# Attention over 16 graphs: ScalarE in written order, and the weights' passes spread over the bursts

## The chip, the core and the metric

The kernel runs on one core of a Trainium2 chip. A core has TensorE (matmul, PE in the profile, with its weight loads as PEld), VectorE (DVE), ScalarE (ACT), GpSimd (POOL), and queues that issue DMA transfers (SP for most of them here). Each engine has its own list of instructions, and semaphores tie the lists together. The metric is the device time of one execution in microseconds (us), from the first to the last instruction, as a median of several executions.

## What is computed

Sixteen graphs of 1024 nodes with 256 features pass through two layers. Only the first layer is touched by the change. For each graph it builds an attention whose queries come from a product with an adjacency matrix weighted by the graph itself:

```python
fea = jnp.transpose(x, (0, 2, 1))
c_adj = jnp.mean(fea, axis=1)                          # mean of a node's features
diff = c_adj[:, None, :] - c_adj[:, :, None]
A = jnp.abs(jnp.abs(jax.nn.sigmoid(diff) - 0.5) - 0.5) * 2.0
A_s = (A + jnp.transpose(A, (0, 2, 1))) * 0.5
Wg = adj[None, :, :] * A_s                             # the graph's weights, 1024 x 1024
g = jax.nn.relu(jnp.einsum('bcn,bnm->bcm', fea, Wg) * para.reshape(1, C, N))
q = jnp.transpose(g, (0, 2, 1)).reshape(B, N, h, hd).transpose(0, 2, 1, 3)
kv = (x @ kv_w).reshape(B, N, 2, h, hd).transpose(2, 0, 3, 1, 4)
attn = jax.nn.softmax(jnp.einsum('bhnd,bhmd->bhnm', q, kv[0]) * scale, axis=-1)
out = jnp.einsum('bhnm,bhmd->bhnd', attn, kv[1])       # 4 heads of 64
# then: x = layernorm(x + out), and a second layer (graph product, two linear
# layers with batch norm, layernorm)
```

All data is float32. With t = tanh(|difference of means| / 2) the weights are (up to the sign, which the kernel puts into the scale of q) `(t - 1) * adj`.

## The kernel before

The first layer is written as a software pipeline. While TensorE works on the attention of graph b, the queries, keys and values of graph b+1 are made between its bursts, and the transposes and first weights of graph b+2. A unit is 128 keys by 512 queries for two heads; a graph has 32 units, and a burst is two of them, so a graph has 16 bursts, numbered u = 0 to 15 below.

```python
with (
    ...
    tc.tile_pool(name="xp", bufs=3) as xp,        # x of three graphs
    tc.tile_pool(name="crp", bufs=1) as crp,
    tc.tile_pool(name="wgp", bufs=NCH) as wgp,    # the 8 weights tiles of one graph
    tc.tile_pool(name="pp", bufs=4) as pp,        # exponentials of four units
    ...
):
# PSUM pools, two tiles each: ps_s (scores), ps_t (everything of the block
# steps, transposes and denominators), ps_o (attention output)
```

The work for a graph's queries, keys and values comes in three lists: `first` (transposes of x), `steps` (block steps: values, keys, graph product) and `side` (the weights' passes).

```python
def prologue(b):
    ...
    def begin():
        ...
        nc.vector.tensor_reduce(csum, xt, AX.X, ALU.add)          # needs x loaded
        ...                                                        # ccol, ncol
        nc.sync.dma_start(c_d[b].rearrange("o (n p) -> p (o n)", p=P), ncol)
        s["crow"] = crp.tile([P, N], F32, tag="crow", name=f"crow_{b}")
        nc.sync.dma_start(s["crow"], c_d[b][0].partition_broadcast(P))

    def transpose_x(c, half):
        if c == 0 and half == 0:
            begin()
        pt = tile_t(f"pxT_{b}_{c}_{half}")
        ...                                                        # 4 transposes
        nc.vector.tensor_copy(s["xT"][:, c, half * HALF : (half + 1) * HALF], pt)

    def weights_abs(n):
        w = wgp.tile([P, N], F32, tag="wg", name=f"wg_{b}_{n}")
        nc.scalar.activation(w, s["crow"], AF.Abs, bias=s["ccol"][:, n : n + 1])
        s["wg", n] = w

    def weights_tanh(n):
        w = s["wg", n]
        nc.scalar.activation(w, w, AF.Tanh, scale=0.5)
        nc.vector.scalar_tensor_tensor(
            w, w, 1.0, adj_s[:, n, :], op0=ALU.subtract, op1=ALU.mult
        )

    def graph_mm(c, half, part):                                   # 2 of 8 matmuls
        ...
        if part == 3:
            q = s["qT"][:, c, hs]
            nc.vector.scalar_tensor_tensor(
                q, ps, -scale, para_s[:, c, hs], op0=ALU.mult, op1=ALU.mult
            )
            nc.scalar.activation(q, q, AF.Relu)

    def keys(kc, half):
        ...
        nc.scalar.copy(s["kT"][:, kc, hs], ps)

    def values(pair):
        ...
        nc.vector.tensor_copy(
            s["v"][:, 2 * pair : 2 * pair + 2, :].rearrange("p n c -> p (n c)"), pt
        )
    ...
    for n in range(NCH):
        side.append((weights_abs, (n,)))
        side.append((weights_tanh, (n,)))
    return first, steps, side
```

A unit's attention is a score product, an exponential on ScalarE, an output product, and a running sum of the exponentials on VectorE:

```python
def scores(i):
    ps = tile_s(f"ps_{i}")
    ...                                                            # 4 matmuls into ps
    p = pp.tile([P, N], F32, tag="p", name=f"p_{i}")
    nc.scalar.activation(p, ps, AF.Exp)

def outputs(i):
    ...                                                            # 4 matmuls with p
    nc.vector.tensor_add(g["acc"], g["acc"], p)                    # first: p0 + p
    if m == NCH - 1:                                               # every 8th unit
        nc.scalar.copy(g["oT"], g["po"][0])
        nc.vector.tensor_add(g["oT"], g["po"][1], g["oT"])

def residual(b, pr, qh):
    ...                                                            # transposes of oT
    nc.vector.tensor_mul(o, ...)                                   # by 1 / denominator
    nc.gpsimd.tensor_tensor(xs, xs, o.rearrange("p n h d -> p n (h d)"), ALU.add)
    if pr == PAIRS - 1 and qh == 1:                                # last of the graph
        layernorm(s["x"], f"l0_{b}")
        nc.gpsimd.dma_start(x1_d[b], s["x"])
        del st[b]
```

The main loop. Inside `manual_schedule` the engines that are named issue in the order of writing; a scheduler orders the others, ScalarE among them.

```python
FULL = {0: 4, 4: 4, 6: 4, 8: 4, 10: 4, 12: 4}
with tc.manual_schedule(engines={mybir.EngineType.PE}):
    ...
    for j in range(len(bursts)):
        b, u = j // PERB, j % PERB
        for i in bursts[j]:
            scores(i)
        run(quarter.get(j, []), 9)                 # denominators
        if u == 0:
            steps, side = next_steps, next_side
            next_first, next_steps, next_side = [], [], []
        if u == 5 and b + 2 < B:
            load_x(b + 2)
            next_first, next_steps, next_side = prologue(b + 2)
        if j:
            back(j - 1)                            # outputs of the burst before
        if u in FULL:
            run(full.get(j, []), 9)                # residuals
            run(steps, FULL[u])
            if u >= 10:
                run(next_first, 2)
        if u > 12:
            run(next_side, 2)
        else:
            run(side, 1 if u in FULL else 2)
```

Of the kernel before, what the change touches and what calls it, by code (L numbers as in the profile page):

```python
# [515 lines left out]
def fast_path(  # L516
# [19 lines left out]
    nc = tc.nc  # L536
# [3 lines left out]
    NCH = N // P  # L540
# [15 lines left out]
    def tile_t(name):  # L556
        return ps_t.tile([P, HALF], F32, tag="t", name=name)
# [4 lines left out]
    x1_d = [dram.tile([P, NCH, C], F32, tag=f"x1_{b}", name=f"x1_{b}") for b in range(B)]  # L562
# [11 lines left out]
    def rsqrt(dst, src, eps):  # L574
        n = dst.shape[1]
        if eps:
            nc.gpsimd.tensor_scalar(dst, src, eps, None, ALU.add)  # L577
            src = dst
        nc.gpsimd.tensor_tensor(dst, src, mhalf[:, :n], ALU.pow)  # L579

    def layernorm(t, name):
        st = small.tile([P, NCH, 6], F32, tag="ln_st", name=f"st_{name}")
        mv = small.tile([P, NCH, 2], F32, tag="ln_mv", name=f"mv_{name}")
        rstd = small.tile([P, NCH], F32, tag="ln_rs", name=f"rs_{name}")
        for n in range(NCH):
            nc.vector.bn_stats(st[:, n, :], t[:, n, :])
            nc.vector.bn_aggr(mv[:, n, :], st[:, n, :])
        rsqrt(rstd, mv[:, :, 1], EPS)
        for n in range(NCH):
            nc.vector.tensor_scalar(  # L590
                t[:, n, :], t[:, n, :], mv[:, n, 0:1], rstd[:, n : n + 1], ALU.subtract, ALU.mult
            )
# [20 lines left out]
    with (  # L613
# [15 lines left out]
        st = {}  # L629

        def load_x(b):
            t = xp.tile([P, NCH, C], F32, tag="x", name=f"x_{b}")
            nc.sync.dma_start(t, x[b].rearrange("(n p) c -> p n c", p=P))
            st[b] = {"x": t}
# [7 lines left out]
        def prologue(b):  # L642


            s = st[b]
            xt = s["x"]
            first, steps, side = [], [], []
# [34 lines left out]
            def weights_tanh(n):  # L682
                w = s["wg", n]
                nc.scalar.activation(w, w, AF.Tanh, scale=0.5)  # L684
                nc.vector.scalar_tensor_tensor(  # L685
                    w, w, 1.0, adj_s[:, n, :], op0=ALU.subtract, op1=ALU.mult
                )
# [57 lines left out]
            for n in range(NCH):  # L745
                side.append((weights_abs, (n,)))
                side.append((weights_tanh, (n,)))
            return first, steps, side


        PAIRS = H // 2
# [8 lines left out]
        def scores(i):  # L760
            b, pr, qh, m = units[i]
            qT, kT = st[b]["qT"], st[b]["kT"]
            ps = tile_s(f"ps_{i}")
            for kh in range(2):
                for hd in range(2):
                    r = slice(hd * D, (hd + 1) * D)
                    ks = slice(m * P + kh * D, m * P + (kh + 1) * D)
                    nc.tensor.matmul(  # L768
                        ps[kh * D : (kh + 1) * D, hd * HALF : (hd + 1) * HALF], kT[r, pr, ks],
                        qT[r, pr, qh * HALF : (qh + 1) * HALF], start=True, stop=True,  # L770
                    )
            p = pp.tile([P, N], F32, tag="p", name=f"p_{i}")
            nc.scalar.activation(p, ps, AF.Exp)  # L773
            A[i] = p

        def outputs(i):
            b, pr, qh, m = units[i]
            s, p = st[b], A.pop(i)
            if m == 0:
                G[b, pr, qh] = {  # L780
                    "po": [tile_o(f"po_{i}_{kh}") for kh in range(2)],
                    "acc": accp.tile([P, N], F32, tag="acc", name=f"acc_{i}"),
                }
            g = G[b, pr, qh]
            for hd in range(2):
                h = 2 * pr + hd
                for kh in range(2):
                    r = slice(kh * D, (kh + 1) * D)
                    nc.tensor.matmul(  # L789
                        g["po"][kh][hd * D : (hd + 1) * D, :], s["v"][r, m, h * D : (h + 1) * D],  # L790
                        p[r, hd * HALF : (hd + 1) * HALF], start=(m == 0), stop=(m == NCH - 1),
                    )
            if m == 0:
                g["p0"] = p
            elif m == 1:
                nc.vector.tensor_add(g["acc"], g.pop("p0"), p)
            else:
                nc.vector.tensor_add(g["acc"], g["acc"], p)  # L798
            if m == NCH - 1:
                k = (b * PAIRS + pr) * 2 + qh  # L800
                g["oT"] = op.tile([P, HALF], F32, tag="oT", name=f"oT_{k}")
                nc.scalar.copy(g["oT"], g["po"][0])
                nc.vector.tensor_add(g["oT"], g["po"][1], g["oT"])
# [25 lines left out]
        def residual(b, pr, qh):  # L829
            g, s = G.pop((b, pr, qh)), st[b]  # L830
            k = (b * PAIRS + pr) * 2 + qh
            nc.vector.reciprocal(r_all[:, k], g["col"])
            pt = tile_t(f"poT_{k}")
            for j in range(4):
                nc.tensor.transpose(
                    pt[:, j * P : (j + 1) * P], g["oT"][:, j * P : (j + 1) * P], ident
                )
            o = rdp.tile([P, 4, 2, D], F32, tag="o", name=f"o_{k}")
            nc.vector.tensor_mul(  # L839
                o, pt.rearrange("p (n h d) -> p n h d", h=2, d=D),  # L840
                r_all[:, k].unsqueeze(3).to_broadcast([P, 4, 2, D]),
            )
            xs = s["x"][:, 4 * qh : 4 * qh + 4, pr * P : (pr + 1) * P]
            nc.gpsimd.tensor_tensor(xs, xs, o.rearrange("p n h d -> p n (h d)"), ALU.add)  # L844
            if pr == PAIRS - 1 and qh == 1:
                layernorm(s["x"], f"l0_{b}")
                nc.gpsimd.dma_start(x1_d[b], s["x"])
                del st[b]

        def run(fs, k):  # L850
            for f, a in fs[:k]:
                f(*a)
            del fs[:k]
# [1 line left out]

        FULL = {0: 4, 4: 4, 6: 4, 8: 4, 10: 4, 12: 4}
        BURST = 2
        bursts = [range(i, i + BURST) for i in range(0, len(units), BURST)]  # L860
        PERB = PER // BURST
        with tc.manual_schedule(engines={mybir.EngineType.PE}):
            load_x(1)
            first, steps, side = prologue(0)
            run(first, 4)
            while steps:
                run(side, 4)
                run(steps, 2)
            next_first, next_steps, next_side = prologue(1)
            run(next_first, 4)  # L870
            run(next_side, 6)
            full, quarter = {}, {}

            def back(j):

                for i in bursts[j]:
                    outputs(i)
                b, pr, qh, m = units[bursts[j][-1]]
                if m == NCH - 1:
                    quarter.setdefault(j + 2, []).append((normalise, (b, pr, qh)))  # L880
                    k = j + 5
                    while k % PERB not in FULL:
                        k += 1
                    full.setdefault(k, []).append((residual, (b, pr, qh)))

            for j in range(len(bursts)):
                b, u = j // PERB, j % PERB
                for i in bursts[j]:
                    scores(i)
                run(quarter.get(j, []), 9)  # L890
                if u == 0:
                    steps, side = next_steps, next_side
                    next_first, next_steps, next_side = [], [], []
                if u == 5 and b + 2 < B:
                    load_x(b + 2)
                    next_first, next_steps, next_side = prologue(b + 2)
                if j:
                    back(j - 1)
                if u in FULL:
                    run(full.get(j, []), 9)  # L900
                    run(steps, FULL[u])
                    if u >= 10:
                        run(next_first, 2)
                if u > 12:
                    run(next_side, 2)
                else:
                    run(side, 1 if u in FULL else 2)
            j = len(bursts)
            back(j - 1)
            for k in range(j, j + 8):  # L910
                run(quarter.get(k, []), 9)
                run(full.get(k, []), 9)

        top = l0c.tile([P, 2], F32, name="top")
        nc.vector.tensor_reduce(top[:, 0:1], r_all, AX.XYZ, ALU.max)
# [275 lines left out]
```

## Time and profile before

| | |
|---|---|
| time, median of 3 | 2997.59 us (2993.03 to 2997.8) |
| span of the profiled execution | 2990.3 us |
| PE busy | 2736.4 us (92%) |
| DVE busy | 1418.0 us (47%) |
| ACT busy | 1138.6 us (38%) |
| POOL busy | 185.7 us (6%) |
| first score matmul of graph 0, last of graph 15 | 81.2 us, 1862.2 us |
| one exponential (L773) x512 | 1018 ns |
| one weights pass on ScalarE: Abs (L679) x128, Tanh (L684) | 1137 ns, 1045 ns |
| one weights product on VectorE (L685) x128 | 1220 ns |
| one running sum (L798) x384 | 1226 ns |

A busy time is the union of an engine's instructions. A row of the profile's slices gives the busy share in tenths for each fortieth of the span. An entry of the timeline gives the start, the length, the engine, the line of the kernel, the operation, and what it writes and reads; in brackets stands how long the engine was idle before it and who released it. Tiles are named as in the kernel: `ps` scores, `p` exponentials, `wg` weights, `pg` the graph product, `pv` and `pk` values and keys, `pxT` the transposes of x.

### The profile page before, as it was taken

The page shows a single profiled execution, that of the slowest core. Times are in us where ns is not written, and L with a number is a line of the kernel's source. Part 1 is how long each engine was busy: PE and PEld are TensorE (multiplying, and loading weights), DVE is VectorE, ACT ScalarE, POOL GpSimd, SP SyncE. Part 2 cuts the span into 40 slices and gives each one's busy share as a digit, 9 for nine tenths or more (in the row PEclk, how much of TensorE's full clock was granted, in tenths as well). Part 3 has the DMA queues.
Part 4 walks back from the last instruction along what each step waited for, and adds up shares of the span by engine and source line. Part 5 has one row for each costly group of instructions (what it writes and reads, how often), then busy time and mean ns, then how long its engine had stood idle before and what let it go on. Part 6 is the DMA issues. An engine that isn't in the chain of part 4 may idle for free. (4 is left out here: it accounts for less than half of the span.)

```text
span 2990.3 us, 32734 instructions
## 1 busy us (share of the span) xinstructions
PE 2736.4 (92%) x13522; PEld 1202.2 (40%) x13522; DVE 1418.0 (47%) x2130; ACT 1138.6 (38%) x1313; POOL 185.7 (6%) x196
## 2 busy tenths in 40 slices
PE   6999999999999999999999999799999999999842
PEld 3433334333333333334333333544444444344432
DVE  3565555655655665655655647511111212233464
ACT  3555354553553553553544535001101111233383
POOL 0000000000000000000000001000000000000032
PEclk9999999999999999999999999699999999999955
DMA  4001101101101001011011010022121220244265
GB/s 134 8 1 36 36 1 36 30 8 36 29 8 37 29 8 37 10 28 36 1 36 36 1 49 24 29 84 112 57 84 71 84 84 32 123 159 150 84 211 198
DMA packets 122062, 169.00 MB, mean 57 GB/s; under 512 B 86704, under 2 KB 103600, under 8 KB 111664
## 3 DMA queue, kind: packets, MB, share of 16 engines
q1 hardware_dynamic: 112720, 99.70, 10.9%
q0 software_dynamic: 9184, 67.12, 5.7%
q8 instruction: 108, 1.77, 0.3%
q14 instruction: 50, 0.41, 0.0%
HBM read 99.36 MB, written 67.44 MB: 56 GB/s over the span
## 5 line engine op out<-in xcount | busy, mean ns | idle before, releaser
L773 ACT ACTIVATE p<-ps 128x1024 f32<-128x1024 f32 x512 | 498.7, 1018 | 275.5 <-PE ps L768 263.6
L768 PE MATMUL ps<-qT,kT 64*64 64x512 f32 x4096 | 519.1, 619 | 69.6 <-ACT p L773 69.6
L798 DVE TENSOR_TENSOR acc<-acc,p 128x1024 f32<-128x1024 f32 x384 | 470.7, 1226 | 187.9 <-ACT p L773 174.8
L789 PE MATMUL po<-p,v 64*64 64x512 f32 x4096 | 500.4, 599 | 0.0
L697 PE MATMUL pg<-wg,x 128*128 128x512 f32 x1024 | 454.4, 597 | 4.3 <-ACT kT L718 4.3
L1003 PE MATMUL pagg<-ahT,x1l 128*128 128x512 f32 x1024 | 444.0, 593 | 0.0
L1022 ACT ACTIVATE hw<-ph,col_b 128x1024 f32<-128x1024 f32 x64 | 71.2, 1113 | 652.7 <-PE ph L1018 652.7
L768 PEld LDWEIGHTS ps<-qT,kT 64*64 64x64 f32 x4096 | 150.9, 137 | 368.1 <-issue 234.2
L1003 PEld LDWEIGHTS pagg<-ahT,x1l 128*128 128x128 f32 x1024 | 194.3, 190 | 241.1 <-issue 241.1
L697 PEld LDWEIGHTS pg<-wg,x 128*128 128x128 f32 x1024 | 190.2, 190 | 246.3 <-issue 216.6
L789 PEld LDWEIGHTS po<-p,v 64*64 64x64 f32 x4096 | 166.3, 137 | 292.8 <-issue 289.6
L1082 PE MATMUL po<-hl,w2T 128*128 128x512 f32 x512 | 222.8, 598 | 6.9 <-ACT hl L1073 6.9
L1018 PE MATMUL ph<-agg,w1T 128*128 128x512 f32 x512 | 222.2, 592 | 0.0
L1007 DVE COPY agg<-pagg 128x1024 f32<-128x1024 f32 x32 | 39.1, 1223 | 377.9 <-PE pagg L1003 377.9
L706 ACT ACTIVATE qT<-qT 128x512 f32<-128x512 f32 x64 | 40.1, 626 | 407.3 <-DVE qT L703 407.3
L685 DVE SCALAR_TENSOR_TENSOR wg<-wg,adj_s 128x1024 f32<-128x1024 f32 x128 | 153.3, 1220 | 77.0 <-ACT wg L684 77.0
L844 POOL TENSOR_TENSOR x<-x,o 128x512 f32<-128x512 f32 x64 | 81.1, 1267 | 1670.3 <-DVE o L839 1670.3
L1024 DVE BATCH_NORM_STATS2 bn_st<-hw 128x6 f32<-128x512 f32 x128 | 82.3, 685 | 152.4 <-ACT hw L1022 152.4
L727 PE MATMUL pv<-kvw_s,xT 128*128 128x256 f32 x512 | 128.0, 394 | 26.8 <-DVE v L731 16.1
L1082 PEld LDWEIGHTS po<-hl,w2T 128*128 128x128 f32 x512 | 98.3, 192 | 131.4 <-issue 121.9
L679 ACT ACTIVATE wg<-crow,ccol 128x1024 f32<-128x1024 f32 x128 | 140.8, 1137 | 17.2 <-PE pg L697 11.9
L1018 PEld LDWEIGHTS ph<-agg,w1T 128*128 128x128 f32 x512 | 97.3, 190 | 122.5 <-issue 122.5
(87 smaller groups left out, 1962.8 us busy)
## 6 DMA issues: line engine op xcount, KB each, us to landing
h<-hw POOLq DMA_DIRECT2D x16, 2048.0 KB, 6.6
hl<-h SPq DMA_DIRECT2D x16, 2048.0 KB
x<-in_x_dram SPq DMA_DIRECT2D x16, 1024.0 KB
x<-x POOLq DMA_DIRECT2D x16, 1024.0 KB, 4.3
x1l<-x SPq DMA_DIRECT2D x16, 1024.0 KB
xf<-x SPq DMA_DIRECT2D x16, 1024.0 KB
out_dram<-xf POOLq DMA_DIRECT2D x16, 1024.0 KB, 5.4
crow<-c SPq DMA_DIRECT2D x16, 512.0 KB
```

The lines of the kernel that those rows point to most:

```text
L679: nc.scalar.activation(w, s["crow"], AF.Abs, bias=s["ccol"][:, n : n + 1])
L685: nc.vector.scalar_tensor_tensor(w, w, 1.0, adj_s[:, n, :], op0=ALU.subtract, op1=ALU.mult)
L697: nc.tensor.matmul(ps, xt[:, n, c * P : (c + 1) * P], s["wg", n][:, hs], start=(n == 0), stop=(n == NCH - 1),)
L727: nc.tensor.matmul(pt[:, j * C : (j + 1) * C], s["xT"][:, c, n * P : (n + 1) * P], kvw_s[:, c, C : 2 * C], start=(c == 0), stop=(c == CC - 1),
L768: nc.tensor.matmul(ps[kh * D : (kh + 1) * D, hd * HALF : (hd + 1) * HALF], kT[r, pr, ks], qT[r, pr, qh * HALF : (qh + 1) * HALF], start=Tr ...
L773: nc.scalar.activation(p, ps, AF.Exp)
L789: nc.tensor.matmul(g["po"][kh][hd * D : (hd + 1) * D, :], s["v"][r, m, h * D : (h + 1) * D], p[r, hd * HALF : (hd + 1) * HALF], start=(m = ...
L798: nc.vector.tensor_add(g["acc"], g["acc"], p)
L1003: nc.tensor.matmul(ps[:, hs], xt[:, m, c * P : (c + 1) * P], ahT[:, m, hs], start=(m == 0), stop=(m == NCH - 1),)
L1018: nc.tensor.matmul(ps[:, hs], w1T[:, c, k * P : (k + 1) * P], t[:, c, hs], start=(c == 0), stop=(c == CC - 1),)
L1024: nc.vector.bn_stats(bn1_st[:, k, 2 * b + half, :], ht[:, k, half * HALF : (half + 1) * HALF])
L1082: nc.tensor.matmul(ps[:, hs], w2T[:, k, c * P : (c + 1) * P], ht[:, k, hs], start=(k == 0), stop=(k == HC - 1),)
```

## The change

ScalarE is added to the engines that issue in the order of writing. So the places at which the weights' passes are written now count, and they are chosen anew: one pass between plain bursts (`SIDE`), and pairs of them between the single block steps of bursts 0 and 4. The product with the adjacency matrix (VectorE) becomes an entry of its own in the list `side`, one weights tile behind the passes. The layer normalisation of a finished graph moves from its last residual to the burst after, ahead of the load of the next x. In bursts 10 and 12 one of the two transposes of x goes ahead of the four graph matmul steps. At the start six entries of `side` are written for each two steps, in place of four. The purpose is to keep passes from standing ahead of exponentials that TensorE waits for.

```diff
@@ weights_tanh
                 nc.scalar.activation(w, w, AF.Tanh, scale=0.5)
+
+            def weights_adj(n):
+                w = s["wg", n]
                 nc.vector.scalar_tensor_tensor(
                     w, w, 1.0, adj_s[:, n, :], op0=ALU.subtract, op1=ALU.mult
                 )
@@ the list side
                 side.append((weights_abs, (n,)))
                 side.append((weights_tanh, (n,)))
+                if n:
+                    side.append((weights_adj, (n - 1,)))
+            side.append((weights_adj, (NCH - 1,)))
@@ residual
-            if pr == PAIRS - 1 and qh == 1:
-                layernorm(s["x"], f"l0_{b}")
-                nc.gpsimd.dma_start(x1_d[b], s["x"])
-                del st[b]
+
+        def finish_x1(b):
+            xt = st.pop(b)["x"]
+            layernorm(xt, f"l0_{b}")
+            nc.gpsimd.dma_start(x1_d[b], xt)
@@ main
-        FULL = {0: 4, 4: 4, 6: 4, 8: 4, 10: 4, 12: 4}
+        FULL = (0, 4, 6, 8, 10, 12)
+        SIDE = {13: 1, 14: 1, 15: 1, 1: 1, 2: 1, 3: 1, 5: 4}
-        with tc.manual_schedule(engines={mybir.EngineType.PE}):
+        with tc.manual_schedule(engines={mybir.EngineType.PE, mybir.EngineType.Activation}):
             ...
             while steps:
-                run(side, 4)
+                run(side, 6)
                 run(steps, 2)
             next_first, next_steps, next_side = prologue(1)
             run(next_first, 4)
-            run(next_side, 6)
-            full, quarter = {}, {}
+            run(next_side, 4)
+            full, quarter, late = {}, {}, {}
@@ back, where the residual is placed in burst k
                     full.setdefault(k, []).append((residual, (b, pr, qh)))
+                    if pr == PAIRS - 1 and qh == 1:
+                        late.setdefault(k + 1, []).append((finish_x1, (b,)))
@@ loop over the bursts
+                if j:
+                    back(j - 1)
+                run(late.get(j, []), 9)
                 if u == 5 and b + 2 < B:
                     load_x(b + 2)
                     next_first, next_steps, next_side = prologue(b + 2)
-                if j:
-                    back(j - 1)
                 if u in FULL:
                     run(full.get(j, []), 9)
-                    run(steps, FULL[u])
                     if u >= 10:
-                        run(next_first, 2)
-                if u > 12:
-                    run(next_side, 2)
+                        run(next_first, 1)
+                    for _ in range(4):
+                        run(steps, 1)
+                        if u <= 4:
+                            run(side, 2)
+                    if u >= 10:
+                        run(next_first, 1)
+                elif u > 12:
+                    run(next_side, SIDE[u])
                 else:
-                    run(side, 1 if u in FULL else 2)
+                    run(side, SIDE.get(u, 0))
             ...
                 run(full.get(k, []), 9)
+                run(late.get(k, []), 9)
```

## The prediction

> **What bounds the kernel now.** I read the engines' busy shares and the clock row first, then the table of stretches, the waits of TensorE, and last the timeline of one graph. The page says where to look:
>
> ```profile
> PE 2736.4 (92%) x13522; PEld 1202.2 (40%) x13522; DVE 1418.0 (47%) x2130; ACT 1138.6 (38%) x1313; POOL 185.7 (6%) x196
> ...
> PE   6999999999999999999999999799999999999842
> ```
>
> TensorE is the bound, but 92% busy hides time: a stretch at half clock counts as busy. So I cut the attention stage into its 16 graphs at the first score matmul of each. Graphs 1 to 13 take 113.9 to 119.3 us, mean 115.4, graph 0 takes 110.6. Graph 14 prepares no successor's weights and takes 105.0. The stretches of graph 8, of graph 14, and of two pieces inside graph 8 (columns: length, busy time of PE, PEld, DVE, ACT, POOL, then clock, DMA share, GB/s):
>
> ```profile
> 1000.83:1115.83 115.00, 108.81 (x692) 44.71 (x688) 68.04 (x92) 55.66 (x64) 7.62 (x7) 0.97 0.09 24
> 1692.62:1797.63 105.01, 103.97 (x676) 42.24 (x672) 50.94 (x74) 39.68 (x48) 7.61 (x7) 1.00 0.12 41
> 1103.57:1109.94 6.37, 1.92 (x21) 0.52 (x13) 4.35 (x5) 6.37 (x9) 0.00 (x0) 0.85 0.08 1
> 1109.94:1114.82 4.88, 4.88 (x24) 1.54 (x28) 4.24 (x6) 2.90 (x3) 0.00 (x0) 0.50 0.00 0
> ```
>
> In the third row TensorE stands while ScalarE is full; in the fourth it works at clock 0.50. ScalarE's timeline tells why:
>
> ```profile
> 1103.95 1.06 ACT L684 ACTIVATE wg<-wg 128x1024 f32<-128x1024 f32 x1
> 1104.91 2.18 ACT L679 ACTIVATE wg<-crow,ccol 128x1024 f32<-128x1024 f32 x2
> 1106.99 1.99 ACT L684 ACTIVATE wg<-wg 128x1024 f32<-128x1024 f32 x2
> 1108.88 1.91 ACT L773 ACTIVATE p<-ps 128x1024 f32<-128x1024 f32 x2
> ...
> 1109.94 3.69 PE L768 MATMUL ps<-qT,kT 64*64 64x512 f32 x16 [4.45 <-ACT p L773]
> ```
>
> Five weights passes stand ahead of the exponentials, so the next scores find no free PSUM tile for 4.45 us. A stall of 4.45 or 4.46 us stands at burst 15 of each of graphs 0 to 13, 14 times.
>
> **What the Trainium skill says.** "TensorE: Matmul & The Clock Gate", section "What's actually happening": the array falls to half clock after an idle window of about 3.4 us and comes back after a busy one; the windows run free. The trace agrees: half-clock pieces are 3.41 or 6.83 us long in this stage. They also follow shorter stalls: one of 2.07 us (graph 2) brought 3.41 us of half clock, one of 1.42 us (graph 5) none. "ScalarE: Activation LUTs", section "Table sets: the hidden batching unit": exp, tanh, abs and relu lie in one set, so interleaving them loads no table. The trace agrees: one table load, 1.28 us, in the whole run. "Perfetto Trace Analysis", section "Sequencer Loop": an engine's instruction waits for its semaphores in the queue, behind it the rest. That makes the order on an engine the thing to read, and I read it in the compiled order of both programs.
>
> **Part 1: weights passes spread out.** A plain burst repeats every 3.43 us (score starts 1020.01, 1023.44). ScalarE spends 1.94 on two exponentials, so 1.5 are free: one pass of 1.05 to 1.14 fits, two don't. The change puts one pass in each of bursts 13, 14, 15, 1 and 2 and the other eleven in the block steps of bursts 0 and 4. In burst 0 TensorE has 7.4 us of block work; ScalarE then has oT copy 0.58, four passes 4.2, two kT copies 1.16, but waits for the first keys. Followed through, the exponentials of burst 1 start 0.5 to 1.0 us late; in burst 4 five passes fit after the keys and those of burst 5 start at about 1037.5 instead of 1035.9. The scores of burst 6 need the first at 1039.2 and it ends at 1038.5: it holds with 0.7 us. So the 14 stalls go: 14 x 4.45 = 62. The half clock after them goes too. In graph 8 it is 4.88 x 0.5 = 2.4; from the spacing of matmul starts in all 14 it is 2.3 in the mean: 14 x 2.3 = 32. Sum 94.
>
> **Part 2: layer normalisation one burst later.** VectorE's order at burst 4 was four statistics, then v; TensorE waited 0.91 us for that v in 14 graphs. In the new order v comes after two of the statistics, so about 0.9 x 14 = 12 us are saved. **Part 3: transposes around the block's graph matmuls.** Two waits of 0.35 us per graph for a PSUM tile disappear, 10 us. In burst 12 the graph matmul takes the tile that the output transposes held, and VectorE frees it only after the exponentials, an add (1.22) and the multiply (0.69), 0.5 us too late: 14 x 0.5 = 7 us lost. **Part 4: the start.** keys' copies now stand behind the first five passes on ScalarE, which wait for crow until 36.46. The first graph matmul moves from 49.0 to about 53, but then runs at full clock; with four passes ahead of the first exponentials I count 4 us lost.
>
> **Part 5: what I expect to be given back.** The lines of graph 8 after burst 4 (VectorE's normalisation, the next x and its sums, qT, then the relu and TensorE's next scores):
>
> ```profile
> 1034.15 2.67 DVE L590 TENSOR_SCALAR x<-x,mv_l,rs_l 128x256 f32<-128x256 f32 x8 [2.12 <-POOL rs_l L579]
> ...
> 1046.62 2.29 DVE L657 TENSOR_REDUCE csum<-x 128x8 f32<-128x2048 f32 x1 [5.61 <-DMA x<-in_x_dram]
> ...
> 1051.55 0.68 DVE L703 SCALAR_TENSOR_TENSOR qT<-pg,para_s 128x512 f32<-128x512 f32 x1
> ...
> 1052.27 0.63 ACT L706 ACTIVATE qT<-qT 128x512 f32<-128x512 f32 x1 [9.12 <-DVE qT L703]
> 1052.81 1.92 ACT L773 ACTIVATE p<-ps 128x1024 f32<-128x1024 f32 x2
> ...
> 1054.20 1.90 PE L768 MATMUL ps<-qT,kT 64*64 64x512 f32 x16
> ```
>
> The x of the second next graph goes into the buffer that the normalised x leaves by DMA. From the last scaling (1036.82) to the start of csum are 9.8 us of store and load. VectorE stands at csum, qT stands behind it, the relu behind qT, and in ScalarE's queue the exponentials of burst 7 behind the relu. The first ends at 1053.81, and the scores of burst 8 come at 1054.20: 0.39 us to spare. In four graphs it was already too late, by 2.07, 1.42, 0.65 and 0.81. The mean end of that exponential is 31.0 us after the graph's burst-4 scores; undisturbed, TensorE comes at 30.75.
>
> The new order makes this chain later and TensorE earlier. Ahead of the last statistics VectorE now has one weights product (1.15) and, between the scalings, a v copy (0.60); with the other places the last scaling moves 2.0 us later. The compiled order keeps qT behind csum in graphs 1 to 13, which have such a load; graph 0's load finds a free buffer. TensorE comes 0.9 earlier (part 2), at 29.85. The new stall is 31.0 + 2.0 + 0.1 - 29.85 = 3.2 us, in graphs 1 to 13: 42. Taken off are the 5 us of such stalls that exist: +37. Stalls of 2.6 to 5 us bring half clock nearly always, some 1.4 us each by the 2.07 one's 3.41 x 0.5 = 1.7 and some misses: 13 x 1.4 - 1.7 = +16.
>
> **Sum.** -94 - 12 - 10 + 7 + 4 + 37 + 16 = -52. Layer 1, from 1863 us on, is not touched; what its start gains or loses I put at zero. 2997.6 - 52 = 2945, rounded with the small waits to 2943.
>
> **Rivals.** (A) The gain stays whole: the chain of part 5 is not shifted, or TensorE's slack covers it. Then -94 - 12 - 10 + 11 = -105, about 2892. For it: DMA times vary, and the idle DVE of 5.6 us before csum looks free. Against: qT and the exponentials are in one order behind it, and four graphs show the stall already. (B) ScalarE in program order becomes the bound: exponentials behind kT copies and passes in bursts 1 and 5 come too late, two stalls of about 1 us per graph: 2943 + 28 = 2971. Against: 0.7 us to spare by my walk, and ScalarE is 56 of 115 us busy. (C) The new stall is as long as the old, 4.5 us and its half clock, and nothing but parts 2 and 3 remains: about 2985. Against: its length follows from a shift of 2.0, not from five passes.
>
> **Range and chances.** The stall's size is the large term: 0.8 us of error is 10 us, the half clock another 9, the start 3. That gives 2915 to 2978 for 8 in 10. 2% is 2937.6, only 5 us below my number, so faster by over 2% gets 0.42, within 2% 0.54, slower 0.04.
>
> **What would show it.** Right: no gap of 4.45 at burst 15; the v wait of 0.9 gone; a gap at burst 8's scores of about 3 us, released by the exponentials, in graphs 1 to 13; graphs of 111 us. Wrong: graphs of 107 us with no gap at burst 8 (then A), or gaps at bursts 2 and 6 (then B), or a csum that starts no later than 23.2 us after burst 4's scores.

## The result, and the profile after

| | before | after |
|---|---|---|
| time, median | 2995.59 us (2993.03 to 2997.80) | 2945.07 us (2944.59 to 2947.85) |
| ratio | 1 | 0.9834, 95% interval 0.9817 to 0.9851 |
| span of the profiled execution | 2990.3 us | 2943.1 us |
| first score matmul of graph 0 | 81.24 us | 87.76 us |
| from there to the last score matmul of graph 15 | 1781.3 us | 1727.8 us |
| from there to the end (layer 1) | 1127.7 us | 1127.6 us |

The change is worth 50 us of 2996, 1.7%. The whole gain lies in the attention stage (-53.6 us); the start gives 6.5 back, and the second layer is as long as it was. The engines' busy shares and TensorE's slices, from the page of the kernel after:

```profile
PE 2713.9 (92%) x13522; PEld 1197.3 (41%) x13522; DVE 1417.3 (48%) x2130; ACT 1146.1 (39%) x1313; POOL 185.7 (6%) x196
...
PE   5999999999999999999999998899999999999842
```

Nothing can be read from these shares: 92% before and 92% after. The waits of TensorE tell more (who waited, for whom; us in total, times, longest). Of the kernel before:

```profile
PE ps L768 <- ACT p L773: 69.6, 20, 4.5
...
PE pv L727 <- DVE v L731: 16.1, 16, 2.9
...
PE pxT L671 <- DVE qT L703: 10.1, 29, 0.3
```

Of the kernel after (the lines have moved: scores are L774, exponentials L779):

```profile
PE ps L774 <- ACT p L779: 39.5, 15, 4.3
...
PE pv L730 <- DVE v L734: 16.4, 29, 1.0
...
PE pg L700 <- DVE o L845: 5.8, 14, 0.4
```

Scores still wait for exponentials, 39.5 us, but at another place. Placed by burst in the timeline, 62.4 of the 69.6 us stood at burst 15 and 6.3 at burst 8; after the change burst 15 has none and burst 8 has 38.5. The waits for `v` are as long in sum and twice as many (2.9 of the 16.1 us before stand at the start, outside the attention stage). The transposes' waits are gone, and a new small one is there for the graph product.

ScalarE's timeline of graph 8 at its end shows why burst 15 is free: one pass between two pairs of exponentials, where five stood together before.

```profile
1079.96 1.94 ACT L779 ACTIVATE p<-ps 128x1024 f32<-128x1024 f32 x2 [0.83 <-PE ps L774]
1081.79 1.06 ACT L684 ACTIVATE wg<-wg 128x1024 f32<-128x1024 f32 x1
1083.34 1.94 ACT L779 ACTIVATE p<-ps 128x1024 f32<-128x1024 f32 x2 [0.49 <-PE ps L774]
```

And the chain behind burst 4 of the same graph, whose burst-4 scores start at 999.00 (VectorE's scalings, the sums, qT; ScalarE's relu and exponentials; TensorE's scores of burst 8):

```profile
1012.16 2.34 DVE L590 TENSOR_SCALAR x<-x,mv_l,rs_l 128x256 f32<-128x256 f32 x7
...
1024.48 2.29 DVE L657 TENSOR_REDUCE csum<-x 128x8 f32<-128x2048 f32 x1 [4.65 <-DMA x<-in_x_dram]
...
1029.26 0.64 DVE L706 SCALAR_TENSOR_TENSOR qT<-pg,para_s 128x512 f32<-128x512 f32 x1
...
1029.93 0.63 ACT L709 ACTIVATE qT<-qT 128x512 f32<-128x512 f32 x1 [11.89 <-DVE qT L706]
1030.47 1.93 ACT L779 ACTIVATE p<-ps 128x1024 f32<-128x1024 f32 x2
...
1031.53 2.01 PE L774 MATMUL ps<-qT,kT 64*64 64x512 f32 x16 [2.25 <-ACT p L779]
```

The scalings end at 1014.5, 15.5 us after the burst-4 scores (13.4 before). The sums start at 25.5 us (23.2 before). TensorE has been ready for 2.25 us when it gets on. Such a stall of 2.1 to 4.3 us stands at burst 8 in each of graphs 1 to 13, in the mean 2.86.

The next table gives it all at once. It is worked out from the timeline: the mean distance from the first score matmul of one burst to that of the next, graphs 1 to 13, in us. Stalls and half clock are both in it. The columns e1 to e9 are experiments below (e4 is within 0.2 of the kernel after in each row, e6 and e7 are as e9 but for burst 12); bursts that don't differ (1, 2, 3, 9, 11, 13) are left out and are 23.36 us in sum.

| burst | before | after | e1 | e2 | e3 | e5 | e8 | e9 |
|---|---|---|---|---|---|---|---|---|
| 0 | 11.41 | 11.89 | 11.43 | 12.68 | 11.92 | 11.80 | 11.80 | 11.32 |
| 4 | 12.20 | 12.04 | 11.40 | 13.75 | 12.94 | 12.11 | 12.13 | 11.29 |
| 5 | 4.47 | 4.34 | 4.42 | 4.47 | 4.51 | 4.34 | 4.34 | 4.34 |
| 6 | 10.61 | 10.61 | 10.61 | 10.61 | 11.44 | 10.61 | 10.61 | 10.61 |
| 7 | 3.93 | 6.52 | 5.23 | 4.08 | 3.95 | 11.05 | 4.73 | 3.48 |
| 8 | 11.18 | 12.18 | 11.23 | 11.07 | 11.06 | 13.14 | 11.23 | 11.00 |
| 10 | 12.05 | 11.44 | 11.44 | 12.05 | 11.44 | 11.44 | 11.44 | 11.44 |
| 12 | 12.44 | 12.55 | 12.55 | 12.44 | 12.55 | 12.55 | 12.55 | 12.44 |
| 14 | 8.09 | 3.43 | 8.15 | 3.43 | 3.43 | 3.43 | 3.43 | 3.43 |
| 15 | 5.71 | 3.43 | 6.12 | 3.43 | 3.43 | 3.43 | 3.43 | 3.43 |
| graph | 115.4 | 111.8 | 116.0 | 111.4 | 110.1 | 117.3 | 109.1 | 106.2 |

Rows 14 and 15 are the stall ahead of burst 15 and its half clock: -6.94 us per graph. Rows 7 and 8 are the new stall ahead of burst 8 and its half clock: +3.59. All other rows together make -0.3.

### The profile page after: what moved, and what is told of

Same layout as the page of the kernel before. It is cut to its first block, busy times and chain, and to the rows that moved or that the text cites. A ratio compares the mean times of both kernels' runs of the same rounds, so it can differ in the third digit from the quotient of the medians.

```text
span 2943.1 us, 32728 instructions
## 1 busy us (share of the span) xinstructions
PE 2713.9 (92%) x13522; PEld 1197.3 (41%) x13522; DVE 1417.3 (48%) x2130; ACT 1146.1 (39%) x1313; POOL 185.7 (6%) x196
## 5 line engine op out<-in xcount | busy, mean ns | idle before, releaser
L779 ACT ACTIVATE p<-ps 128x1024 f32<-128x1024 f32 x512 | 497.0, 1020 | 166.1 <-PE ps L774 156.1
L774 PE MATMUL ps<-qT,kT 64*64 64x512 f32 x4096 | 504.9, 604 | 39.5 <-ACT p L779 39.5
L774 PEld LDWEIGHTS ps<-qT,kT 64*64 64x64 f32 x4096 | 148.8, 133 | 328.3 <-issue 243.5
L688 DVE SCALAR_TENSOR_TENSOR wg<-wg,adj_s 128x1024 f32<-128x1024 f32 x128 | 164.7, 1295 | 32.2 <-ACT wg L684 32.2
L706 DVE SCALAR_TENSOR_TENSOR qT<-pg,para_s 128x512 f32<-128x512 f32 x64 | 43.6, 681 | 259.1 <-PE pg L700 259.1
L730 PE MATMUL pv<-kvw_s,xT 128*128 128x256 f32 x512 | 128.1, 394 | 33.4 <-DVE v L734 16.4
L679 ACT ACTIVATE wg<-crow,ccol 128x1024 f32<-128x1024 f32 x128 | 147.6, 1153 | 0.0
```

What stands on the lines that cost most here:

```text
L688: nc.vector.scalar_tensor_tensor(w, w, 1.0, adj_s[:, n, :], op0=ALU.subtract, op1=ALU.mult)
L730: nc.tensor.matmul(pt[:, j * C : (j + 1) * C], s["xT"][:, c, n * P : (n + 1) * P], kvw_s[:, c, C : 2 * C], start=(c == 0), stop=(c == CC - 1),
L774: nc.tensor.matmul(ps[kh * D : (kh + 1) * D, hd * HALF : (hd + 1) * HALF], kT[r, pr, ks], qT[r, pr, qh * HALF : (qh + 1) * HALF], start=Tr ...
```

## The experiments

The theory to test: the written order of ScalarE takes the stalls of burst 15 away, and the late normalisation puts a shorter one at burst 8, because VectorE's sums wait for a transfer with qT behind them. The rivals: the gain comes from the places of the passes or from the other parts, not from the order; or the stall at burst 8 is ScalarE's own, full as it is in program order. Each experiment was timed against the kernel before; ratios carry their 95% interval.

### e1: all but the written order of ScalarE

```diff
 # from the kernel after
-        with tc.manual_schedule(engines={mybir.EngineType.PE, mybir.EngineType.Activation}):
+        with tc.manual_schedule(engines={mybir.EngineType.PE}):
```

> The changed kernel with ScalarE left to the scheduler, all else as changed. Theory (the written order of ScalarE takes the passes from in front of the exponentials of burst 14): the compiled order again has six passes between the exponentials of bursts 13 and 14, so the gap of 4 to 5 us at burst 15 comes back in 14 graphs with its half clock, and the gap at burst 8 stays at about 2 us: 2985 to 3010 us. Rival (the gain comes from the moved layer normalisation and the transposes): the time stays near 2945.

Measured: 2997.44 us, 1.0006 (0.9997 to 1.0015). The whole gain is gone. The scheduler packs five passes together again at the old place (ScalarE's and TensorE's timeline, graph 8, burst 15):

```profile
1111.25 2.20 ACT L679 ACTIVATE wg<-crow,ccol 128x1024 f32<-128x1024 f32 x2
1113.34 2.00 ACT L684 ACTIVATE wg<-wg 128x1024 f32<-128x1024 f32 x2
1115.23 1.15 ACT L679 ACTIVATE wg<-crow,ccol 128x1024 f32<-128x1024 f32 x1
1116.27 1.01 ACT L779 ACTIVATE p<-ps 128x1024 f32<-128x1024 f32 x1
...
1117.34 3.84 PE L774 MATMUL ps<-qT,kT 64*64 64x512 f32 x16 [4.54 <-ACT p L779]
```

So the new places in the program do nothing while a scheduler is free to ignore them. Two more things are in column e1: row 7 is 1.3 longer than before, so part of the stall at burst 8 comes without ScalarE's written order; and row 4 is 0.8 shorter: `v` comes earlier, as predicted for the normalisation's new place, but only here (e1 moves other places too, so this is not shown for the normalisation alone).

### e2: nothing but the written order of ScalarE

```diff
 # from the kernel before; all passes at their old places
-        with tc.manual_schedule(engines={mybir.EngineType.PE}):
+        with tc.manual_schedule(engines={mybir.EngineType.PE, mybir.EngineType.Activation}):
```

> The kernel before with only ScalarE added to the engines in written order; the passes stay at their old places, two between plain bursts, and the layer normalisation stays where it was. Theory: two passes between bursts overrun a plain burst by 0.6 us, which the slack of about 1.3 us absorbs for two bursts, so the gap at burst 15 shrinks from 4.45 to under 1 us; the chain from store to load to sums is not later, so burst 8 is as before (0.4 us in the mean); the start loses about 5 us: 2905 to 2925. Rival (one pass at a time is what the written order needs): stalls of 0.6 us or more at each of bursts 14, 15, 2, 3, over 40 us in all: 2945 or more.

Measured: 2946.06 us, 0.9835 (0.9818 to 0.9851). I had expected 20 to 40 us less. This one word is worth as much as the whole change. Burst 15 has no stall, and burst 8 nearly none (8.0 us in all graphs together, one piece of half clock in the stage). What it loses stands in rows 0 and 4: `v` comes late, 33.9 us of waits in these two bursts, and another 14.7 for `o`. VectorE's and TensorE's timeline, graph 8, burst 4:

```profile
996.39 1.22 DVE L685 SCALAR_TENSOR_TENSOR wg<-wg,adj_s 128x1024 f32<-128x1024 f32 x1
...
1002.25 0.66 DVE L731 COPY v<-pv 128x512 f32<-128x512 f32 x1
...
1002.96 2.00 PE L727 MATMUL pv<-kvw_s,xT 128*128 128x256 f32 x8 [1.58 <-DVE v L731]
```

A weights product stands ahead of the last sum, `o` and the statistics, and `v` behind them all; in the kernel before no product stood there. So the switch on ScalarE has moved VectorE's products too; that the scheduler does so because it reckons with other ends of the passes is my reading, and no run shows it. Neither the theory nor the rival had this: the rest of the change is worth nothing in sum because it wins here (rows 0, 4, 5 and 10: 3.2 us per graph shorter than e2) what it loses at burst 8 (rows 7 and 8: 3.6 longer).

### e3: the normalisation back at its old place

```diff
 # from the kernel after, in back()
-                        late.setdefault(k + 1, []).append((finish_x1, (b,)))
+                        full.setdefault(k, []).append((finish_x1, (b,)))
```

> The changed kernel with the layer normalisation and the store of the finished graph put back behind the last residual (burst 4 in place of 5). In VectorE's compiled order the weights product then falls into the idle time before the scalings, and all scalings come in one piece, as before the change. Theory (the gap at burst 8 is the chain scaling, store, load, sums, qT, relu, exponential, which the change made 2 us later): last scaling back at 13.4 to 14.0 us after burst 4's scores, gap at burst 8 down from 2.9 us to about 0.4 in the mean and its half clock gone, 13 x 3.4 = 45 us: 2895 to 2910. Rival 1 (the gap is ScalarE's written order, late exponentials in bursts 1 and 5 passed on): unchanged, 2945. Rival 2 (VectorE has too much to do between bursts 4 and 8): unchanged or slower, 2945 to 2955.

Measured: 2921.67 us, 0.9748 (0.9732 to 0.9764). The mechanism is right, the size short. The stalls at burst 8 fall from 38.5 to 6.5 us and the half clock of the stage from eight pieces to none. But the last scaling ends 14.7 to 16.3 us after the burst-4 scores, not at 13.4 to 14.0, as a weights product (1.19 us, at 991.64) stands ahead of them, and rows 4 and 6 get longer. Row 6 shows no idle TensorE at all. The wait stands at the weight loads (PEld), in VectorE's and PEld's timeline of graph 8:

```profile
994.72 2.67 DVE L590 TENSOR_SCALAR x<-x,mv_l,rs_l 128x256 f32<-128x256 f32 x8 [1.89 <-POOL rs_l L579]
997.31 0.69 DVE L734 COPY v<-pv 128x512 f32<-128x512 f32 x1
...
998.05 0.14 PEld L819 LDWEIGHTS den<-acc,ones 64*64 64x64 f32 x3 [0.81 <-DVE v L734]
```

The second denominator tile takes the PSUM tile that `v` leaves, and `v` stands behind eight scalings. Denominators use quarters of the array (64 by 64). The records of the output product, which uses quarters too, start at 998.07, while denominators still start at 998.53, and PE shows no gap. So I read it thus: some quarters go on while others wait, and the loss comes out at the graph product, which needs all four. Row 6 is 0.83 us longer. The kernel after splits the scalings, and `v` goes between the first and the second.

### e4: a fourth buffer for x

```diff
 # from the kernel after; two statistics tiles change their pool to make room
-        tc.tile_pool(name="xp", bufs=3) as xp,
+        tc.tile_pool(name="xp", bufs=4) as xp,
```

> The changed kernel with a fourth buffer for x (and the batch norm statistics moved to another pool, to make room). Theory: in the compiled order the scheduler uses the buffer to load one graph further ahead, so the sums at the same place of VectorE's order are those of the next graph but one more, and their load again waits for the store of the same burst: gap at burst 8 unchanged, 2940 to 2950. Rival (the load has a buffer free, so the sums find their x there): gap gone, 2895 to 2910.

Measured: 2944.29 us, 0.9827 (0.9809 to 0.9845), nothing. The stall at burst 8 stays, 36.0 us. With one more buffer the scheduler lets the sums of one graph later take the same place in VectorE's order, so they wait for the same transfer. A buffer shortens a wait only if the order behind it stays.

### e5: sums that wait for no load

From graph 3 on the sums are taken over the keys of the graph before in place of x. This leaves out the true means, so the weights are other numbers; all else is done.

```diff
 # from the kernel after, in begin()
-                nc.vector.tensor_reduce(csum, xt, AX.X, ALU.add)
+                src = xt
+                if b > 2:
+                    src = st[b - 1]["kT"].rearrange("p c (k n) -> p (c k) n", n=C)
+                nc.vector.tensor_reduce(csum, src, AX.X, ALU.add)
```

> The changed kernel, but from graph 3 on the sums (csum) read the keys of the graph before instead of the freshly loaded x: same shape, same duration, no load to wait for. It leaves out the true node means (the weights are then those of other data); the layer normalisation, the store and the load stay where the change put them. Theory (burst 8's gap is VectorE standing at csum for a load): csum waits for nothing; what stays late is the reciprocal, whose column comes through the same transfer queue behind the load, so the gap at burst 8 shrinks from 2.9 us to 0.5 to 1.5 us, half clock gone: 2897 to 2915 us. Rival (VectorE has too much work between bursts 4 and 8, or ScalarE's order is late by itself): gap unchanged, 2940 to 2950.

Measured: 3016.21 us, 1.0068 (1.0052 to 1.0085): worse than the kernel before, and my theory as it stood fell. The sums no longer wait (they start some 9 us earlier), yet the stall at burst 8 is 7.38 us in the mean of graphs 1 to 13. SP's, VectorE's and TensorE's timeline of graph 8:

```profile
1062.17 0.38 SPq L665 DMA_DIRECT2D c<-ncol  x1
1064.93 0.93 SPq L833 DMA_DIRECT2D dcol<-den  x2
...
1074.46 0.20 DVE L841 RECIPROCAL r_all<-dcol 128x8 f32<-128x8 f32 x1 [9.81 <-DMA dcol<-den]
...
1076.85 3.69 PE L777 MATMUL ps<-qT,kT 64*64 64x512 f32 x16 [7.41 <-ACT p L782]
```

Another instruction that waits for a transfer stands ahead of qT: the reciprocal of the denominators. Its column `dcol`, two transfers of 2 KB, was issued from 1064.93 on, but 2.8 us ahead of it the means' 4 KB `c` had been issued, since the sums were done so early, and the reciprocal could start only 9.5 us later. In the kernel after the order is the other way round: `dcol` at 1024.65, `c` at 1028.08.

### e8: the same without the means' write

As e5, and from graph 3 on the means aren't written, and `crow` is read from those of graph 2. This leaves out a 4 KB write per graph besides the true means.

```diff
 # from e5, in begin()
-                nc.sync.dma_start(c_d[b].rearrange("o (n p) -> p (o n)", p=P), ncol)
+                if b < 3:
+                    nc.sync.dma_start(c_d[b].rearrange("o (n p) -> p (o n)", p=P), ncol)
-                nc.sync.dma_start(s["crow"], c_d[b][0].partition_broadcast(P))
+                nc.sync.dma_start(s["crow"], c_d[min(b, 2)][0].partition_broadcast(P))
```

> As the run with sums over other data, and from graph 3 on the sums are no longer written to memory either (crow is loaded again from graph 2's). It leaves out the true node means. In the run before it the reciprocal ahead of qT waited 9.8 us, for two columns that came through the queue behind the 9 us write of the sums. Theory (the gap at burst 8 is whatever stands ahead of qT in VectorE's order waiting for a transfer): with that write gone the columns land some 3 us after their issue, at about 28 us after burst 4's scores, and the gap at burst 8 is 0.5 to 1.5 us: 2897 to 2915 us. Rival (VectorE's work between bursts 4 and 8 is too much in itself): gap of 2.5 us or more, 2940 or more.

Measured: 2909.52 us, 0.971 (0.9694 to 0.9727), as expected; the stall at burst 8 is 1.06 us in the mean of graphs 1 to 13. VectorE's and TensorE's timeline of graph 8:

```profile
1005.23 0.20 DVE L842 RECIPROCAL r_all<-dcol 128x8 f32<-128x8 f32 x1 [3.20 <-DMA dcol<-den]
...
1007.62 2.01 PE L778 MATMUL ps<-qT,kT 64*64 64x512 f32 x16 [0.80 <-ACT p L783]
```

The same column now lands 2.8 us after its issue (1002.39). The read of `crow` (512 KB) has moved as well, since it no longer waits for the write: it is issued at 989.97, ahead of the column. In e5 it was issued at 1072.46, 7.5 us behind the column, so it can't have held the column for those 7.5 us. So both halves are shown: the small write was what held the column in e5, and what is left of the stall is the reciprocal's wait. In the kernel after, the two waits lie one upon the other and the sums' is the longer one.

### e6: VectorE too in written order

The logical end of it: nothing that waits for a transfer is written ahead of qT. The statistics go to bursts 2 and 6, the scalings and the next load to burst 7, the sums to burst 10, the denominators' add behind the running sums.

```diff
 # from the kernel after; normalise_sum, x1_stats and x1_scale (parts of normalise and finish_x1) are not shown
-        with tc.manual_schedule(engines={mybir.EngineType.PE, mybir.EngineType.Activation}):
+        with tc.manual_schedule(engines={mybir.EngineType.PE, mybir.EngineType.Activation,
+                                         mybir.EngineType.DVE}):
@@ back
-                    if pr == PAIRS - 1 and qh == 1:
-                        late.setdefault(k + 1, []).append((finish_x1, (b,)))
+                    if pr == PAIRS - 1:
+                        late.setdefault(k + 2, []).append((x1_stats, (b, qh)))
+                        if qh == 1:
+                            late.setdefault(k + 3, []).append((x1_scale, (b,)))
@@ loop over the bursts
+                run(sums.get(j, []), 9)          # add of the denominators' halves
-                if u == 5 and b + 2 < B:
+                if u == 7 and b + 2 < B:
```

> The changed kernel with VectorE too in written order, and places written for it: statistics of the finished graph in bursts 2 and 6, scalings, store and next load in burst 7, sums at burst 10 where they stand in the text, the denominators' sum behind the running sums. Theory: qT no longer stands behind csum, so the gap at burst 8 goes, and v is copied as soon as it is there, so the gaps at bursts 0 and 4 go; graphs 1 to 13 at 106.5 us instead of 111.8: 2865 to 2890 us. Rival (VectorE in written order meets its own heads of queue, the denominators' copy above all): new gaps of 1 us or more in several bursts, 2900 or more.

Measured: 2895.58 us, 0.9668 (0.9652 to 0.9684), 6 us above the expected range. Graphs 1 to 13 take 107.2 us each, all the same, with no stall at burst 8 and no wait for `v`. Two losses remain: the graph product of burst 12 waits 1.32 us for `o` (14 times, 18.5 us), and graph 0 takes 118.3, since the passes for graph 1 stand in order ahead of its exponentials and wait for `crow`.

### e7: a start of its own

```diff
 # from e6
-            while steps:
-                run(side, 6)
-                run(steps, 2)
+            run(steps, 8)                        # values and keys
+            run(side, 24)                        # all passes of graph 0
+            run(steps, 8)
             next_first, next_steps, next_side = prologue(1)
             run(next_first, 4)
-            run(next_side, 4)
+            run(steps, 4)
+            run(next_side, 2)
+            run(steps, 4)
+            run(next_side, 2)
```

> As the kernel with VectorE in written order, and the start written anew: values and keys of graph 0 first, then its weights' passes, then the graph products, the next graph's transposes and first passes between them. Theory (the change's start lost time because the keys' copies stood behind five passes that wait for crow): first score matmul at 79 to 82 us instead of 87.8, 6 to 8 us less than the kernel with VectorE in written order: 2858 to 2883. Rival (the start is bound by the loads, whatever the order): no difference over 3 us.

Measured: 2876.3 us, 0.9602 (0.9586 to 0.9618). The time is as expected, but not the way: the first score matmul comes at 87.5, not at 79 to 82. The gain is graph 0, 103.5 us in place of 118.3. The start is held by the transfer of `crow` and by the passes, one weights tile per 2.1 us.

### e9: both transposes of burst 12 behind the graph product

```diff
 # from e7
-                    if u >= 10:
+                    if u == 10:
                         run(next_first, 1)
 ...
                     if u >= 10:
-                        run(next_first, 1)
+                        run(next_first, u - 10 or 1)
```

> As the kernel in written order with its own start, but in burst 12 both transposes of the next x stand behind the graph matmuls, as before the change. Theory (the 1.32 us there is the graph matmul waiting for the PSUM tile that the output transposes hold until VectorE has multiplied): the graph matmul takes the other tile and doesn't wait, a wait of 0.35 us for qT comes back: 14 x 0.97 = 13.6 us less, 2858 to 2868. Rival (the wait moves to the next instruction): unchanged, 2873 to 2880.

Measured: 2861.51 us, 0.9546 (0.953 to 0.9562), the best of all, 2.8% below the kernel after. The stretches of its graph 8 and its graph 14 (length, then PE, PEld, DVE, ACT, POOL busy, clock, DMA share, GB/s), and the same two of the kernel after:

```profile
931.89:1038.05 106.16, 105.78 (x692) 44.23 (x688) 68.11 (x91) 55.94 (x65) 7.61 (x7) 1.00 0.10 26
1568.88:1672.78 103.90, 103.87 (x677) 42.42 (x672) 64.95 (x92) 53.35 (x62) 7.61 (x7) 1.00 0.12 42
```

```profile
975.78:1085.66 109.88, 106.11 (x692) 44.03 (x688) 67.62 (x92) 56.09 (x65) 7.62 (x7) 1.00 0.09 25
1645.20:1750.54 105.34, 104.03 (x676) 42.22 (x672) 63.44 (x91) 53.49 (x62) 7.61 (x7) 1.00 0.12 41
```

In graph 8 of e9 TensorE is busy for 105.78 of 106.16 us; what is left is one wait of 0.35 for a transpose's tile. From here this stage is shortened by taking work from TensorE.

## Why the prediction was right

2943 was predicted, 2945 measured. The mechanism of the gain and of the new stall holds. That the number agrees to 2 us is partly luck: the terms for `v`, `o` and the start came out 18 us worse than predicted, the others 8 better, and 5 us of the gain are in none of them. Measured terms are differences of waits in the attention stage; the half clock is from the granted-clock record of both traces, half of the busy time within its pieces. The waits for `v` hold 1.8 us of gaps of 0.13 in burst 0 of the kernel before, too short for the table of waits.

| term, us | predicted | measured |
|---|---|---|
| 14 stalls at burst 15 | -62 | -62.4 |
| half clock, old pieces off, new ones on | -32 + 16 | -18.1 (32.5 to 14.4) |
| new stalls at burst 8, net | +37 | +32.2 (6.3 to 38.5) |
| waits for `v` | -12 | +1.4 (15.0 to 16.4) |
| waits for `o` in bursts 0 and 4 | not foreseen | +2.5 |
| transposes | -10 | -9.8 |
| graph product of burst 12 | +7 | +5.8 |
| start | +4 | +6.5 |
| second layer | 0 | -0.1 |

These add up to -42; the span went down by 47.2. The 5 us between lie in no wait; ends of matmuls are modelled, and I leave them open.

**Part 1, right.** No gap at burst 15; e1 shows that the order does it, e2 that nothing else is needed. ScalarE's walk held: the exponentials of burst 5 were expected 14.1 us after the burst-4 scores, and start at 14.4, in time for burst 6. Rival B, ScalarE as the bound, has nothing for it: no stall at bursts 2 and 6 in any graph.

**Part 2, wrong.** The step "v comes after two of the statistics, so about 0.9 x 14 = 12 us are saved" failed. The place is as predicted: `v` does stand behind two statistics only (VectorE: statistics at 1005.62, `v` at 1006.29). But I counted positions from the sums on and took the sums' start as given. A weights product (1.22 us, at 998.81) now stands ahead of them, as ScalarE's passes finish in bursts 1 to 3, and in burst 0 even two. So `v` starts 7.3 us after the burst-4 scores, and in e1, where no product stands there, at 7.0. VectorE's timeline of graph 8, of the kernel before and of the kernel after:

```profile
1029.75 0.75 DVE L586 BATCH_NORM_STATS2 st_l<-x 128x6 f32<-128x256 f32 x2 [0.78 <-POOL x L844]
...
1031.29 0.66 DVE L731 COPY v<-pv 128x512 f32<-128x512 f32 x1
```

```profile
998.81 1.22 DVE L688 SCALAR_TENSOR_TENSOR wg<-wg,adj_s 128x1024 f32<-128x1024 f32 x1
...
1005.62 0.75 DVE L586 BATCH_NORM_STATS2 st_l<-x 128x6 f32<-128x256 f32 x2 [0.79 <-POOL x L850]
1006.29 0.67 DVE L734 COPY v<-pv 128x512 f32<-128x512 f32 x1
```

The mean wait is 0.58 in burst 4 (0.91 before) and 0.55 in burst 0 (0.13 before); in e1 it is 0.11 and 0.15.

**Parts 3 and 4, right, sizes apart.** The transposes' waits went, the graph product's came at 0.42 in place of 0.5. At the start ScalarE's first pass comes 3.4 us later than before (39.88 against 36.46): `crow` itself is there 2.1 us later, and the table load, which ran at 0.73 us before, now stands behind the first pass's wait for `crow` and costs its 1.28 us. The first graph matmul comes at 57.3, predicted 53. I had read only the order of passes and copies.

**Part 5, right.** "The new stall is 3.2 us, in graphs 1 to 13": it is 2.86 there. In graph 8 the last scaling moved by 2.1 us, predicted 2.0, and the csum starts at 25.5, later than the 23.2 of before. In the mean of graphs 1 to 13 the releasing exponential ends 33.46 us after the burst-4 scores, predicted 33.1. The stall is shorter all the same, mostly by part 2's error once more: "TensorE comes 0.9 earlier (part 2), at 29.85"; as `v` saved 0.3 us in burst 4 and not 0.9, it came at 30.66 in the mean (in graph 8 at 30.28, 1031.53 - 2.25 - 999.00). So the error stands twice in the sum, with opposite signs. e3 shows the normalisation's place as its cause (-32 us of stalls there), e5 and e8 that the chain is wider than I wrote. Not the sums alone, but every instruction ahead of qT in VectorE's order that waits for a transfer can hold it. Rival A would have needed an order with none of them; e6 is the first such kernel, with graphs of 107.2 us, and e9 the last, at 2862. Rival C's 4.5 us stall is seen in no graph, though three reach 4.2 to 4.3.

Of the 105 us that rival A counts, 47 were given back at burst 8 in a new wait (32 of stall, 14 of half clock) and 16 at `v` and `o`.

## What to carry to other kernels

A switch that puts one engine into written order also moves what the other engines' scheduler does, so read the compiled order of all of them, and test the switch alone before you rewrite the places around it: here it was worth the whole change. In a list that an engine works off in order, an instruction that waits for a transfer must not stand ahead of one that the bounding engine waits for; another buffer doesn't help while the order stays. Busy shares show none of this (92% and 92%); the distance from burst to burst does.

## What the runs showed of the hardware that I had not expected

- **A stall's place in the clock's windows tells whether half clock follows.** Thirteen stalls at burst 8 of the kernel after, of 2.12 to 4.33 us, brought eight pieces of half clock, of 3.41 or 6.83 us: one after each of the seven stalls of 2.57 us and more, and of the six shorter ones only after the shortest, 2.12, not after those of 2.25 to 2.37. In e1 stalls of 2.58 and 2.72 us brought none, so the length alone does not tell. The Trainium skill, "TensorE: Matmul & The Clock Gate", section "What's actually happening", says that the windows of about 3.4 us run free. The traces agree: in each of the eleven, all changes of the granted clock lie on one grid of 3.41 us. Laid over that grid, the stall of 2.12 us falls whole into one window, while the five of 2.25 to 2.37 and the two of e1 lie across a border, with at most 1.91 us of idle TensorE in one window. The attention stages have 5430 such windows at full clock in all. After every window with 2.00 us or more of idle time in it, 62 of them, half clock followed; after none with 1.93 or less, but for two in graph 15. (The ends of matmuls are modelled, so these limits are good to some hundredths at best.)
- **4 KB can be slow.** The means' write `c`, from 128 partitions with eight values of four bytes each into one row of 1024, takes long: the read of `crow` that waits for it is issued 9.2 to 12.1 us later in graphs 1 to 13 of the kernel after. Two transfers of 2 KB issued 2.8 us behind it took 9.5 us, without it 2.8 (e5, e8). "DMA: Bandwidth & Descriptors", section "Specifications", says that below 512 B a transfer doesn't reach line rate and is a read-modify-write; the direction agrees, but no run here tells how much of the time comes from it.
- **A wait can cost time without idle time of PE.** In e3 a wait of 0.81 us, which I take to be that of some quarters of TensorE, shows as no idle time of PE, only at PEld, and the burst with the next product that uses the whole array is 0.83 us longer.
